# A two-layer graph kernel on one core: weights' block sums on one engine at a time, c on ScalarE, h sums in another order

## The chip, the core and the metric

The kernel runs on one core of a Trainium2 chip. A core has a matrix engine (TensorE, PE in the profile) and three engines that work element by element: VectorE (DVE), ScalarE (ACT) and GpSimd (POOL). SyncE (SP) issues most transfers. Each engine works through its own queue in the order in which the program gives it instructions, and waits for another engine only by semaphores. The metric is the device time of one execution in microseconds (us); "before" is the median of three runs.

## What is computed

The input `x` holds 128 batches of a 128 x 512 matrix. `adj` is a 128 x 128 matrix, mostly zeros.

```python
# layer 0
h = max(layernorm(x), 0)
A = adj @ h; C = A + b                            # (batch, 128, 512)
pre = A[:, :, None, :] + (C - A)[:, :, :, None]
x = x + max over the last axis of relu(pre)       # cut: comes to x + relu(rowmax(A) + b)
# layer 1
h = max(layernorm(x), 0)
q, k, v = h @ Wq + bq, h @ Wk + bk, h @ Wv + bv   # 8 heads of 64
w = softmax(q k^T / 8, masked where adj == 0)
x = x + w @ v
```

The step of layer 0 adds to each row of `x` one number, which the kernel calls `c`; layernorm takes away what is constant in a row, so both layers use the same `h`, and `c` is only added to the result.

## The kernel before

The batches are worked in 32 groups of four (`G = 4`, `NG = 32`). For each group PE makes the scores of the group, its `v`, and the `q` and `k` of the next group, then the attention of the group. The three projections are done in the manner of Strassen and Winograd: `h` and the weights are cut in quarters, sums of quarters are formed, and seven products take the place of eight. Most of these seven are cut once more in the same way, so that sums of blocks of 128 x 128 are needed too.

Sums of the weights are made once, in the beginning. A `weight_blocks` of one `k` is four additions of 128 x 128; there are five `k` for each of the three weights.

```python
def weight_blocks(eng, n, ks=(3, 2, 0, 1, 4)):
    for k in ks:
        ...                                        # (cut) a: a quarter or sum, s: the four results
        for o, x, op, y in (
            (s[0], a[:, 1, 0], ALU.add, a[:, 1, 1]),
            (s[2], s[0], ALU.subtract, a[:, 0, 0]),
            (s[1], a[:, 0, 0], ALU.subtract, a[:, 1, 0]),
            (s[3], a[:, 0, 1], ALU.subtract, s[2]),
        ):
            eng.tensor_tensor(o, x, y, op=op)      # L422
```

Sums of `h` are made for every group. `h_sum(g, k)` is one of four subtractions over quarters (512 columns): `t3 = b22 - b12`, `t1 = b12 - b11`, `t2 = b22 - t1`, `t4 = b21 - t2` for k = 0 to 3. `h_blocks(g, k, parts)` forms, on GpSimd, the block sums of one of `t4 b22 b21 t1 t3` (k = 0 to 4) in three parts; part 0 has 256 columns, parts 1 and 2 have 128.

```python
eng.tensor_tensor(HB[g][o], HB[g][a], HB[g][b], op=ALU.subtract)     # h_sum, L379
nc.gpsimd.tensor_tensor(o, x, y, op=ALU.subtract)                    # h_blocks, L396
```

The number `c` of a batch is made from the row maximum of its adjacency product; `add_bv` adds the bias of `v` to `x` on GpSimd, and `add_c` adds `c` on ScalarE.

```python
def maximum(m):
    g, i = divmod(m, G)
    nc.vector.reduce_max(AMAX[g][:, i : i + 1], PA[m], axis=AX.X)    # L352
    if i == G - 1:
        nc.vector.tensor_scalar(C[g], AMAX[g], b0_sb, 0.0, op0=ALU.add, op1=ALU.max)   # L354

def norm_end(m, bv=True):
    nc.scalar.activation(HN[m], x_of(m), AF.Relu, scale=RSTD[m], bias=NMR[m])          # L308
    if m >= G and bv:
        add_bv(m)                                                    # L314, GpSimd
```

The products of one projection of one group stand in six rows, and after each row come the other engines' tasks of that row (`todo`). `first`, `sixth`, `seventh` and `inner` are matmuls of blocks on PE (L587); what ends in `_to` is the DVE work that takes their results out of PSUM (L639, L665); `end...` is DVE or ScalarE work that finishes a product of quarters (L517, L521, L527).

```python
def steps(p, tail, mid, t3):
    t = tail + [lambda: None] * 8
    return [
        [t[0], p.p1],
        [call(p.first, 5, True), call(p.first_to, 5), t[1], call(p.p6a, (0,)), ...],       # cut
        [call(p.first, 2, True), call(p.seventh, 7), call(p.seventh_to, 7), call(p.terms7, 0), mid,
         call(p.inner, 2), p.end2, call(p.inner, 5), call(p.first43), call(p.first_to, 2),
         call(p.first_to, 4),
         call(p.inner, 7), t3, call(p.terms7, 1)],
        [p.end7, p.end5],
        [call(p.sixth, 2), call(p.sixth_to, 2), call(p.sixth, 4), call(p.sixth, 3), call(p.sixth_to, 4)],
        [call(p.inner, 4), call(p.inner, 3), call(p.seventh, 2), call(p.seventh, 4),
         call(p.seventh, 3), call(p.seventh_to, 2), call(p.seventh_to, 4), p.end4],
    ]
```

`p6a` is the product that uses `t2`. The `v` of group 0 and of group 31 and the first `k` are done without the second cut: seven products of quarters, each eight matmuls of 256 columns (L481), in the order `p1, p6, p2, p7, p5, p4, p3`; `p7` waits until DVE's `end6` (L517) has read the bank of `p6`, `p4` in the same way for `end7` (L517), `p3` for `end5` (L527).

The beginning and the tasks of a group:

```python
weight_sums(nc.gpsimd, "v")                      # four sums over 512 columns, L434
plain_q(0, 0)
weight_sums(nc.vector, "k")
...                                              # cut: norms, adjacency, plain_q, products of the first k
weight_sums(nc.gpsimd, "q")
weight_blocks(nc.gpsimd, "q", (3,))
for g in range(NG):
    ...                                          # cut
    add(4, h_sum, g + 1, k)                      # k = 1, 2; on VectorE
    for k, i in ((4, 0), (4, 1), (3, 0), (3, 1)):
        add(4, h_blocks, g + 1, k, (i,))
    add(5, h_sum, g + 1, 3, nc.gpsimd)
    for k, i in ((2, 0), (3, 2), (2, 1), (2, 2), (0, 0), (1, 0), (4, 2)):
        add(5, h_blocks, g + 1, k, (i,))
    ...                                          # cut
    if g == 0:
        for s, k in enumerate((3, 2, 0, 1, 4)):
            add(s, weight_blocks, nc.vector, "k", (k,))
        for s, k in ((0, 2), (0, 0), (1, 1)):
            add(s, weight_blocks, nc.vector, "q", (k,))
        for s, k in ((0, 3), (0, 2), (1, 0), (1, 1), (2, 4)):
            add(s, weight_blocks, nc.vector if k in (3, 2) else nc.gpsimd, "v", (k,))
        add(3, weight_blocks, nc.gpsimd, "q", (4,))
        for i in range(G):
            add((3, 3, 3, 11)[i], add_bv, i)
```

Of the kernel before, what the change touches and what calls it, by code (L numbers as in the profile page):

```python
# [53 lines left out]
G = 4  # L54
# [115 lines left out]
def tile_adj_preln_d2(  # L170
# [42 lines left out]
    def fast(ctx):  # L213
# [136 lines left out]
        def maximum(m):  # L350
            g, i = divmod(m, G)
            nc.vector.reduce_max(AMAX[g][:, i : i + 1], PA[m], axis=AX.X)  # L352
            if i == G - 1:
                nc.vector.tensor_scalar(C[g], AMAX[g], b0_sb, 0.0, op0=ALU.add, op1=ALU.max)  # L354

        def adjacency(m):
            product(m)
# [338 lines left out]
                    return  # L696
                self.add_blocks(k, 1, slice(0, 2), 7)

        def steps(p, tail, mid, t3):

            t = tail + [lambda: None] * 8
            return [
                [t[0], p.p1],
                [call(p.first, 5, True), call(p.first_to, 5), t[1], call(p.p6a, (0,)),
                 call(p.first, 7, True), call(p.first_to, 7), call(p.p6a, (1, 2)),
                 call(p.sixth, 5), call(p.sixth_to, 5), call(p.sixth, 7), call(p.sixth_to, 7),
                 call(p.p6a, (3,)), call(p.seventh, 5), call(p.seventh_to, 5), p.end6],
                [call(p.first, 2, True), call(p.seventh, 7), call(p.seventh_to, 7), call(p.terms7, 0), mid,
                 call(p.inner, 2), p.end2, call(p.inner, 5), call(p.first43), call(p.first_to, 2),
                 call(p.first_to, 4),  # L710
                 call(p.inner, 7), t3, call(p.terms7, 1)],
                [p.end7, p.end5],
                [call(p.sixth, 2), call(p.sixth_to, 2), call(p.sixth, 4), call(p.sixth, 3), call(p.sixth_to, 4)],
                [call(p.inner, 4), call(p.inner, 3), call(p.seventh, 2), call(p.seventh, 4),
                 call(p.seventh, 3), call(p.seventh_to, 2), call(p.seventh_to, 4), p.end4],
            ]

        def later(p):
# [2 lines left out]
        def call(m, *a):  # L721
            return lambda: m(*a)
# [119 lines left out]
        with tc.manual_schedule():  # L842
# [11 lines left out]
            adjacency(1)  # L854
            transposes(2)
            transposes(3)
            weight_sums(nc.gpsimd, "v")
            plain_q(0, 0)
            weight_sums(nc.vector, "k")
# [1 line left out]
                h_sum(0, k)  # L861
            adjacency(2)
            norm(G)
            norm_end(G)
            plain_q(0, 1)
            norm(G + 1)
            norm_end(G + 1)
            adjacency(3)
            plain_q(1, 0)
            blocks(G)  # L870
            blocks(G + 1)
            move(G + 1)
            plain_q(1, 1)
            k = Products(0, "k")
            more = {
# [5 lines left out]
            for s, p in enumerate((k.p1, k.p6, k.p2, k.p7, k.p5, k.p4, k.p3)):  # L881
                p()
                for f, m in more.get(s, ()):
                    f(m)
            weight_sums(nc.gpsimd, "q")
            weight_blocks(nc.gpsimd, "q", (3,))
            for g in range(NG):
                b = g * G
                if g > 0:
# [3 lines left out]
                for p in [Products(g, "v")] + [Products(g + 1, n) for n in "qk" if g + 1 < NG]:  # L893
                    if p.n == "v" and g in (0, NG - 1):
                        part += [
                            [p.p1], [p.p6], [p.p2], [p.p7], [p.p5], [p.p4, p.p3],
                        ]
                        continue
                    t3 = mid = lambda: None
                    if p.n == "v":  # L900
                        t3 = lambda: h_sum(g + 1, 0, nc.gpsimd)
                    if p.n == "q":
                        mid = lambda: [
                            h_blocks(g + 1, k, (i,)) for k, i in ((0, 1), (1, 1), (0, 2), (1, 2))
                        ]
                    part += steps(p, tail, mid, t3)
                    tail = later(p)
                    if p.n == "k":
                        part[-1] += tail
                        tail = []  # L910
# [6 lines left out]
                if g + 1 < NG:  # L917
# [9 lines left out]
                        add(0, adjacency, m - 1)  # L927
                    if g == 0:
                        add(3, h_sum, 1, 0)
                    for k in (1, 2):  # L930
                        add(4, h_sum, g + 1, k)
                    for k, i in ((4, 0), (4, 1), (3, 0), (3, 1)):
                        add(4, h_blocks, g + 1, k, (i,))
                    add(5, h_sum, g + 1, 3, nc.gpsimd)
                    for k, i in ((2, 0), (3, 2), (2, 1), (2, 2), (0, 0), (1, 0), (4, 2)):
                        add(5, h_blocks, g + 1, k, (i,))
                    if g + 2 < NG:
                        for s, l in next_norms(m).items():
# [25 lines left out]
                for s, ps_ in enumerate(part):  # L964
                    for p in ps_:
                        p()
# [51 lines left out]
```

## Time and profile before

| what | value |
|---|---|
| median of 3 runs | 1506.74 us |
| lowest and highest | 1502.37 and 1508.06 us |
| span of the profiled execution | 1497.8 us |
| PE busy | 1473.3 us, 98% |
| POOL busy | 1317.3 us, 88% |
| DVE busy | 1217.8 us, 81% |
| ACT busy | 652.7 us, 44% |

A row of a timeline has the start in us from the beginning of the span, the duration in us, the engine, the line of the kernel, the operation, what it writes and reads, the shapes and how many equal instructions are merged into the row. In brackets stand the engine's idle time before the row and what ended it. A matmul of float32 appears as two instructions. Matmuls overlap in the pipe, so the distance of two starts tells what one costs PE, and the duration of a row is longer than that. A row of windows has the stretch, its length, then for each engine its busy time and its number of instructions, then the clock, the share of the DMA engines and what they moved.

### The profile page before, as it was taken

To read this page: it belongs to the slowest core of one execution; us is meant where nothing else is said; L and a number is where in the kernel's file an instruction comes from. 1 tells how busy PE (TensorE), PEld (TensorE's weight loads), DVE (VectorE), ACT (ScalarE), POOL (GpSimd) and SP (SyncE) were. 2 spreads that over 40 slices of the span, in tenths; PEclk is the share of its full clock that TensorE was granted. 3 is DMA by queue.
4 is the path that set the end of the run, shared out by engine and by line. 5 is a ranking of instruction groups with operands and counts; after the bars stand their busy time and mean duration, and the time that the engine had idled before them with its cause. 6 is when DMAs were issued, how large, how long until landed. Compare 5 with 4: busy or idle time off the path is not lost.

```text
span 1497.8 us, 38618 instructions
## 1 busy us (share of the span) xinstructions
PE 1473.3 (98%) x14565; PEld 1336.5 (89%) x14565; DVE 1217.8 (81%) x3016; ACT 652.7 (44%) x1455; POOL 1317.3 (88%) x1564
## 2 busy tenths in 40 slices
PE   8899999999999999999999999999999999999997
PEld 6789998999898999999998999999999989999987
DVE  6988877888788888788887888887888878888877
ACT  3344444444544444444445444444444454444432
POOL 5799899899898898998988988989989889889882
PEclk9999999999999999999999999999999999999999
DMA  5231223312223212233122232122332222331211
GB/s 172 48 86 27 75 76 82 86 37 70 76 77 86 66 43 77 75 83 86 30 76 74 79 86 70 40 78 75 82 86 40 67 74 77 86 79 33 63 42 59
DMA packets 307836, 105.67 MB, mean 71 GB/s; under 512 B 273152, under 2 KB 273280, under 8 KB 307648
## 3 DMA queue, kind: packets, MB, share of 16 engines
q1 hardware_dynamic: 307328, 102.84, 26.6%
q8 instruction: 117, 1.92, 0.5%
q14 instruction: 71, 0.58, 0.1%
q0 software_dynamic: 176, 0.27, 0.1%
q10 hardware_dynamic: 144, 0.07, 0.0%
HBM read 37.03 MB, written 33.55 MB: 47 GB/s over the span
## 4 chain that ended last, share of the span: by engine, by line
PE 93%; DVE 3%; POOL 2%; issue 1%; DMA 0%; ACT 0%; SPq 0%; DVEq 0%; POOLq 0%
PE bk L587 47%; PE bk L481 22%; PE bk L786 8%; PE bk L756 8%; PE bk L348 7%; PE bk L732 1%; POOL h L396 1%; DMA xp<-in_x_dram 0%; DVE ssk_sb L422 0%; POOL w L768 0%; POOL xp L314 0%; POOL o L816 0%; POOL u L690 0%; DVE ssq_sb L422 0%; DVE amax L352 0%
## 5 line engine op out<-in xcount | busy, mean ns | idle before, releaser
L768 POOL TENSOR_TENSOR w<-w,live 128x512 f32<-128x512 f32 x248 | 308.5, 1276 | 0.0
L690 POOL TENSOR_TENSOR u<-u,t 128x512 f32<-128x512 f32 x184 | 234.4, 1274 | 82.0 <-DVE t L639 57.0
L764 ACT ACTIVATE w<-bk 128x512 f32<-128x512 f32 x256 | 128.8, 628 | 276.3 <-PE bk L756 276.3
L665 DVE TENSOR_TENSOR u<-u,bk 128x256 f32<-128x256 f32 x552 | 206.5, 415 | 43.6 <-PE bk L587 26.6
L639 DVE TENSOR_TENSOR u<-u,bk 128x128 f32<-128x128 f32 x368 | 109.0, 316 | 81.8 <-PE bk L587 80.8
L816 POOL TENSOR_TENSOR o<-xp,o 128x512 f32<-128x512 f32 x122 | 151.8, 1277 | 20.1 <-DVE RS L803 20.1
L314 POOL TENSOR_TENSOR xp<-xp,bv_sb 128x512 f32<-128x512 f32 x128 | 159.4, 1278 | 3.7 <-ACT hn L308 3.7
L308 ACT ACTIVATE hn<-xp,nmr,rstd 128x512 f32<-128x512 f32 x124 | 100.5, 811 | 137.4 <-POOL nmr L305 82.4
L352 DVE TENSOR_REDUCE amax<-bk 128x1 f32<-128x512 f32 x128 | 86.6, 677 | 77.2 <-PE bk L348 77.2
L508 ACT COPY u<-bk 128x512 f32<-128x512 f32 x95 | 55.0, 579 | 184.0 <-PE bk L481 176.2
L348 PE MATMUL bk<-hn,adjT 128*128 128x512 f32 x248 | 126.9, 593 | 0.0
L786 PE MATMUL bk<-v,w 128*64 128x65 f32 x4096 | 126.5, 223 | 0.0
L786 PEld LDWEIGHTS bk<-v,w 128*64 128x64 f32 x4096 | 122.1, 138 | 4.1 <-issue 0.3
L756 PE MATMUL bk<-qT,kT 64*128 64x128 f32 x2048 | 123.0, 275 | 0.0
L756 PEld LDWEIGHTS bk<-qT,kT 64*128 64x128 f32 x2048 | 116.8, 188 | 2.5 <-issue 0.3
L587 PE MATMUL bk<-ssv_sb,h 128*128 128x128 f32 x720 | 111.7, 277 | 0.3 <-DVE u L665 0.3
L587 PEld LDWEIGHTS bk<-ssv_sb,h 128*128 128x128 f32 x720 | 98.6, 192 | 14.5 <-issue 13.9
L804 DVE TENSOR_TENSOR o<-bk,RS 128x448 f32<-128x448 f32 (+1 forms) x161 | 93.7, 582 | 5.5
L812 ACT ACTIVATE xp<-xp,c 128x512 f32<-128x512 f32 x128 | 91.2, 715 | 5.3 <-POOL xp L314 5.3
L321 DVE STREAM_TRANSPOSE tb<-hn 128x512 f32<-128x512 f32 x124 | 87.0, 702 | 2.4 <-ACT hn L308 2.4
L396 POOL TENSOR_TENSOR h<-hT,h 128x128 f32<-128x128 f32 x186 | 83.7, 457 | 4.9
L587 PEld LDWEIGHTS bk<-h,ssq_sb 128*128 128x128 f32 x558 | 74.7, 192 | 14.9 <-issue 7.2
(201 smaller groups left out, 4101.4 us busy)
## 6 DMA issues: line engine op xcount, KB each, us to landing
out_dram<-o SPq DMA_DIRECT2D x128, 256.0 KB, 2.4
xp<-in_x_dram SPq DMA_DIRECT2D x62, 512.0 KB, 5.1
hT<-tb SPq DMA_DIRECT2D x992, 32.0 KB, 1.9
xp<-in_x_dram SPq DMA_DIRECT2D x4, 256.0 KB, 4.1
wq_sb<-in_L_gnn_Wq_dram SPq DMA_DIRECT2D x2, 512.0 KB, 7.5
wk_sb<-in_L_gnn_Wk_dram SPq DMA_DIRECT2D x2, 512.0 KB, 9.5
wv_sb<-in_L_gnn_Wv_dram SPq DMA_DIRECT2D x2, 512.0 KB, 10.5
bv_sb<-in_L_gnn_bv_dram POOLq DMA_DIRECT2D x1, 256.0 KB, 6.8
```

The lines of the kernel that those rows point to most:

```text
L314: nc.gpsimd.tensor_tensor(x_m, x_m, bv_sb, op=ALU.add)
L348: nc.tensor.matmul(PA[m], adjT, HN[m], start=True, stop=True)
L481: nc.tensor.matmul(bank[:, r, :], lhs, rhs, start=first and i == 0, stop=i == 3, skip_group_check=True,)
L587: nc.tensor.matmul(out, lhs, rhs, start=start, stop=True, skip_group_check=True)
L639: nc.vector.tensor_tensor(to, to, what.to_broadcast(to.shape), op=ALU.add)
L665: nc.vector.tensor_tensor(to, to, what, op=ALU.add)
L690: nc.gpsimd.tensor_tensor(u, u, T7, op=ALU.add)
L756: nc.tensor.matmul(psc[j][:, f, :], KT[g][r, f, i * D : (i + 1) * D], QT[g][r, f, i * D : (i + 1) * D], start=True, stop=True,)
L764: nc.scalar.activation(w[:, j], psc[j], AF.Exp, scale=HD ** -0.5)
L768: eng.tensor_tensor(w[:, j], w[:, j], live_h, op=ALU.mult)
L786: nc.tensor.matmul(pav[r, c : c + HE], w[:, h % 2, h // 2, r], V[:, i, h, :], start=True, stop=True,)
L816: eng.tensor_tensor(y, x_of(b), y, op=ALU.add)
```

## The change

The changed kernel computes the same with the same instructions but for `c`; it moves them to other engines and places.

- **Weights' block sums.** Those of `v` are now all on VectorE, in the beginning, beside the products of the first `k`. Those of `k` stay on VectorE beside the `v` products of group 0, and those of `q` are all on GpSimd. They are to share the element engines better, and no stretch is to have sums of all three weights at once.
- **Bias additions.** `add_bv` of batches 0 to 3 goes to the beginning, ahead of the sums of Wv on GpSimd; that of batches 4 and 5 goes behind the first products.
- **c on ScalarE.** One activation (Relu with bias) takes the place of VectorE's `tensor_scalar`.
- **Second sum of h.** `h_sum(g + 1, 2)`, which makes `t2`, goes from row 4 to a place just ahead of `end4` in the last row of `v`, behind `seventh_to`, so that VectorE empties PE's bank first.
- **GpSimd's block sums.** All three parts of `b21` (k = 2) come ahead of `t4 = b21 - t2`, since `t2` comes later.
- **The last full group.** In group 30, where no adjacency products are left, `first43` is issued before `inner(5)`.

```diff
-                nc.vector.tensor_scalar(C[g], AMAX[g], b0_sb, 0.0, op0=ALU.add, op1=ALU.max)
+                nc.scalar.activation(C[g], AMAX[g], AF.Relu, bias=b0_sb)
...
-                 call(p.inner, 2), p.end2, call(p.inner, 5), call(p.first43), call(p.first_to, 2),
-                 call(p.first_to, 4),
+                 call(p.inner, 2), p.end2] + [call(p.inner, 5), call(p.first43)][::-1 if late else 1] +
+                [call(p.first_to, 2), call(p.first_to, 4),
...
-                 call(p.seventh, 3), call(p.seventh_to, 2), call(p.seventh_to, 4), p.end4],
+                 call(p.seventh, 3), call(p.seventh_to, 2), call(p.seventh_to, 4)] + ([t2, p.end4] if p.n == "v" else [p.end4]),
...
+            for m in range(G):
+                add_bv(m)
             weight_sums(nc.gpsimd, "v")
...
             blocks(G)
+            weight_blocks(nc.vector, "v", (3, 2, 0))
             blocks(G + 1)
             move(G + 1)
+            weight_blocks(nc.vector, "v", (1, 4))
...
+                if s < 2:
+                    add_bv(G + s)
+                elif s < 6:
+                    weight_sum(nc.gpsimd, "q", s - 2)
-            weight_sums(nc.gpsimd, "q")
-            weight_blocks(nc.gpsimd, "q", (3,))
+            weight_blocks(nc.gpsimd, "q", (3, 2))
...
+                        t2 = lambda: h_sum(g + 1, 2)
...
-                    part += steps(p, tail, mid, t3)
+                    part += steps(p, tail, mid, t2, t3, g == NG - 2)
...
-                    for k in (1, 2):
-                        add(4, h_sum, g + 1, k)
+                    add(4, h_sum, g + 1, 1)
+                    if g == 0:
+                        add(4, h_sum, 1, 2)
...
+                    add(5, h_blocks, g + 1, 2)
                     add(5, h_sum, g + 1, 3, nc.gpsimd)
-                    for k, i in ((2, 0), (3, 2), (2, 1), (2, 2), (0, 0), (1, 0), (4, 2)):
+                    for k, i in ((0, 0), (1, 0), (3, 2), (4, 2)):
                         add(5, h_blocks, g + 1, k, (i,))
...
-                    for s, k in enumerate((3, 2, 0, 1, 4)):
+                    add(0, weight_blocks, nc.gpsimd, "q", (0, 1, 4))
+                    for s, k in ((0, 3), (0, 2), (1, 0), (1, 1), (3, 4)):
                         add(s, weight_blocks, nc.vector, "k", (k,))
-                    for s, k in ((0, 2), (0, 0), (1, 1)):
-                        add(s, weight_blocks, nc.vector, "q", (k,))
-                    for s, k in ((0, 3), (0, 2), (1, 0), (1, 1), (2, 4)):
-                        add(s, weight_blocks, nc.vector if k in (3, 2) else nc.gpsimd, "v", (k,))
-                    add(3, weight_blocks, nc.gpsimd, "q", (4,))
-                    for i in range(G):
-                        add((3, 3, 3, 11)[i], add_bv, i)
```

More of the change, by code (lines that the diff above doesn't have):

```diff
@@ L697, in seventh_to, with steps @@
                 self.add_blocks(k, 1, slice(0, 2), 7)
-        def steps(p, tail, mid, t3):
+        def steps(p, tail, mid, t2, t3, late):
             t = tail + [lambda: None] * 8
@@ L863, in fast @@
             norm(G)
-            norm_end(G)
+            norm_end(G, False)
             plain_q(0, 1)
             norm(G + 1)
-            norm_end(G + 1)
+            norm_end(G + 1, False)
             adjacency(3)
@@ L898, in fast @@
                         continue
-                    t3 = mid = lambda: None
+                    t2 = t3 = mid = lambda: None
                     if p.n == "v":
+                        t2 = lambda: h_sum(g + 1, 2)
                         t3 = lambda: h_sum(g + 1, 0, nc.gpsimd)
```

## The prediction

> **What bounds the kernel now.** I read the page's busy shares and the chain that ended last first, then a table of windows cut at the first score matmul (L756) of each group of four batches, then the timelines of the stretches that stood out.
>
> ```profile
> PE 1473.3 (98%) x14565; PEld 1336.5 (89%) x14565; DVE 1217.8 (81%) x3016; ACT 652.7 (44%) x1455; POOL 1317.3 (88%) x1564
> ...
> PE 93%; DVE 3%; POOL 2%; issue 1%; DMA 0%; ACT 0%; SPq 0%; DVEq 0%; POOLq 0%
> ```
>
> TensorE (PE) is the bound: a saving elsewhere counts only where PE waits for it. The windows show where that is: columns are the stretch, its length, then busy time by engine.
>
> ```profile
> 44.39:96.14 51.75, 46.21 (x427) 40.75 (x427) 48.10 (x113) 19.74 (x43) 43.67 (x64) 1.00 0.18 40
> 96.14:142.69 46.55, 45.87 (x462) 41.54 (x458) 38.62 (x95) 20.59 (x46) 41.60 (x50) 1.00 0.27 69
> 142.69:188.34 45.65, 45.61 (x463) 41.65 (x459) 37.38 (x95) 20.48 (x46) 41.61 (x50) 1.00 0.29 71
> 1378.04:1423.68 45.64, 45.60 (x463) 41.63 (x459) 37.36 (x95) 20.48 (x46) 41.60 (x50) 1.00 0.24 59
> ```
>
> A group takes 45.64 us when nothing disturbs it. The first costs 51.75 us, 6.1 more, and in it DVE is busy 48.10 of them. From the starts of the other groups' first score matmuls, most intervals are 45.63 to 45.69; six are longer: 46.55, 46.03, 46.63, 46.67 and twice 45.88.
>
> In the first group, on PE:
>
> ```profile
> 51.72 1.89 PE L481 MATMUL bk<-wv_sb,hT 128*128 128x256 f32 x8
> 55.55 1.97 PE L481 MATMUL bk<-sv_sb,hs 128*128 128x256 f32 x8 [1.94 <-DVE u L517]
> ...
> 61.60 2.00 PE L481 MATMUL bk<-wv_sb,hs 128*128 128x256 f32 x8 [1.50 <-DVE u L517]
> 64.98 1.97 PE L481 MATMUL bk<-sv_sb,hT 128*128 128x256 f32 x8 [1.39 <-DVE v L527]
> ...
> 71.58 0.69 PE L587 MATMUL bk<-h,wq_sb 128*128 128x128 f32 x4 [0.71 <-DVE u L639]
> ```
>
> Eight such matmuls issue in 1.73 us (50.00 to 51.72), so the row at 55.55 starts 2.10 us late (51.72 + 1.73 = 53.45). In the same way 61.60 is 1.66 late, 64.98 is 1.65 late and 71.58 is 0.88 late. The sum is 6.3 us. Each waits for a DVE instruction that stands in DVE's queue behind the weights' block sums (L422). The L517 that releases 55.55 ran at 54.73, after 20 block sums without a gap from 47.28 to 54.73: 0.37 us each.
>
> **What the Trainium skill says.** The page "SBUF — State Buffer", section "Who interferes with whom": VectorE and GpSimd share a pair of SBUF ports under an exclusive lock; a VectorE tensor_scalar that runs on two ports, and a VectorE instruction with two SBUF inputs against a GpSimd one that reads SBUF, block or are blocked; PE and ScalarE wait for nobody. The trace agrees. `c` is a tensor_scalar over 4 columns: 0.229 us at best, 0.534 median, 1.82 at worst, each time beside GpSimd work:
>
> ```profile
> 103.53 1.82 DVE L354 TENSOR_SCALAR c<-amax,b_sb 128x4 f32<-128x4 f32 x1
> ...
> 101.55 3.73 POOL L816 TENSOR_TENSOR o<-xp,o 128x512 f32<-128x512 f32 x3
> ...
> 105.59 0.49 PE L587 MATMUL bk<-wv_sb,h 128*128 128x128 f32 x2 [0.64 <-DVE u L639]
> ```
>
> It ends when GpSimd's run ends (101.55 + 3.73 = 105.28), and PE pays. Block sums of 128x128 have two SBUF inputs: 0.28 us alone, 0.4 to 0.6 beside GpSimd, up to 1.35 beside its 512-column additions. Second place: the page "ScalarE: Activation LUTs", section "Rules for kernel authors", budgets about 0.3 us for an activation with a pointer bias plus 0.83 ns per element; for 4 columns that is an estimate of 0.3 us, and no run so far shows this shape. Relu already runs in this kernel, whose one table load is at the beginning.
>
> **Part 1, the weights' block sums.** There are 60 (three weights, five sets of four). Before, DVE did 40 of them in the congested stretch and GpSimd 20. Now GpSimd does the 20 of q, DVE does the 20 of k there, and DVE does the 20 of v earlier, between 26 and 31.6 us. There DVE has room: it is idle from 26.5 to 28.9 and from 29.6 to 31.6, 4.4 us; GpSimd is idle then too, so the 20 should run at about 0.21 us each (the spacing of the rows at 47.81 and 48.01), 4.2 us. They fit; PE, which runs without a wait from 13 to 44 us, should not notice. In the v products DVE then has 8 k-sums (about 3 us with contention, 46.2 to 49.2) before its first L517, which PE makes ready at 51.7: no wait. The later k-sums, 8 and then 4, lie in the 1.7 us or more between PE's deadlines. GpSimd gives up seven bias additions (1.28 us each) to earlier idle time and gets the 12 remaining q-sums until about 58.4; the additions to `x` of batches 0 to 3 fill its wait for Wv up to 16.85. The q products begin near 61 instead of 66.78, so the h block sums on GpSimd, from 58.4, still keep ahead. All four waits should go: 6.3 us, of which I count 6.0.
>
> **Part 2, c on ScalarE.** Half a microsecond of DVE per group is free on most groups, since PE doesn't wait there. It counts in the three with 1.8 us: 46.55, 46.63 and 46.67 less 45.64 is 0.91, 0.99 and 1.03. Sum 2.9; I count 2.7. ScalarE is idle there (its copy at 102.42 ends at 103.0, the next starts at 104.18).
>
> **Part 3, the second sum of h.** On the way from v to q, in every group:
>
> ```profile
> 158.95 0.83 DVE L379 TENSOR_TENSOR hT<-hT 128x512 f32<-128x512 f32 x1
> 159.81 0.83 DVE L379 TENSOR_TENSOR hs<-hT 128x512 f32<-128x512 f32 x1
> 160.57 0.41 DVE L639 TENSOR_TENSOR v<-v,bk 128x256 f32<-128x256 f32 x1
> 160.90 0.74 DVE L665 TENSOR_TENSOR u<-u,bk 128x256 f32<-128x256 f32 x2
> ...
> 161.34 0.44 PE L587 MATMUL bk<-h,wq_sb 128*128 128x128 f32 x2
> 161.82 0.46 PE L587 MATMUL bk<-hT,sq_sb 128*128 128x128 f32 x2
> ...
> 173.88 0.38 PE L587 MATMUL bk<-h,wk_sb 128*128 128x128 f32 x2
> 174.10 0.39 PE L587 MATMUL bk<-hT,sk_sb 128*128 128x128 f32 x2
> ```
>
> From q to k the pair of rows stands 0.22 apart; from v to q it stands 0.48 apart. The second row writes the scratch bank that L639 and L665 read, and these end at 161.64 because both h sums stand before them. With the second sum (159.81) behind them they end near 160.9, ahead of PE. That returns 0.26 us in 30 groups (1 to 30), 7.8 at most. But the sum now ends near 161.63, and its result `t2` feeds the product at 162.11, which moves up to 161.85: only 0.2 us remains for the semaphore. I count 0.2 x 30 = 6.0.
>
> **Part 4, GpSimd's other order.** The sums of `b21` come before `t4` since `t4` needs `t2`; same instructions, same sum. The last sum that inner(5) of q needs, (3,2), moves from 164.06 to about 166.0, and its matmul is at 166.74 before: 0.4 us in hand after the shift. I count 0, with a risk.
>
> **Part 5, the last full group.** Two waits for DVE L665 (1437.67 and 1462.37) make PE 0.45 us late each, since no adjacency product stands there to fill the time. Issuing first43 before inner(5) puts three matmuls (0.67 us) between. I count 0.9. The waits for GpSimd there (0.5) may stay.
>
> **Sum.** 6.0 + 2.7 + 6.0 + 0.9 = 15.6; less 0.8 for small waits that I can't place (part 4's above all): 14.8. 1506.7 - 14.8 = 1491.9.
>
> **Rivals.** First, part 3 gives nothing: `t2` becomes the wait, because DVE's sum is stretched beside GpSimd (0.83 instead of 0.69 already, 0.99 at one place), or (3,2) arrives late. For it speaks the 0.2 us margin; against it that the lost time is then at most what it was. Result 1506.7 - 8.8 = 1497.9, and with 0.1 us of new wait in each group 1501. Second, the waits of the beginning move rather than go: q's sums, all on GpSimd and slowed by DVE's k-sums at its side, delay the h block sums, and PE waits for GpSimd at 61 to 68 us. GpSimd is busy 43.67 of the first 51.75 us, so it has about 2 us to spare in 45.7. Half of part 1 would be lost: about 1495. Third, GpSimd becomes the bound: busy 41.6 of 45.4 us, with room of 3.8 us per group and its waits for DVE inside that; I give it little.
>
> **Range and chances.** The best sum, 6.3 + 2.9 + 7.8 + 1.5, is 18.5 and gives 1488; rivals one and two together give about 1501. The three times before spread over 5.7 us, so 1485 to 1500 should hold it 8 times in 10. For faster by over 2% it would need under 1476.6, twice the sum that PE's waits allow: 0.03. Slower by over 2% would need a new wait of 1 us in every group: 0.02. Within 2%: 0.95.
>
> **What would show it.** First interval of score matmuls 45.7 to 46.2 (before 51.75) and no PE row in it with a wait for L517; `c` on ACT near 0.2 to 0.3 us and no interval above 46; a plain group at 45.38 to 45.45 with the v-to-q pair 0.22 apart; the group before the last 0.9 shorter. I am wrong if the product with `t2` or inner(5) of q starts late in every group, if PE waits for GpSimd L396 in the first group, or if the early v-sums hold back DVE so that PE waits before 44 us.

## The result and the profile after

| | before | after |
|---|---|---|
| median | 1505.72 us (1502.37 to 1508.06, 4 runs) | 1493.96 us (1492.89 to 1494.99, 4 runs) |
| span of the profiled execution | 1497.8 us | 1491.1 us |
| first interval of score matmuls | 51.75 us | 45.23 us |
| a plain interval | 45.64 us | 45.75 us |

The ratio is 0.9923, with a 95% interval of 0.9902 to 0.9945: 11.8 us less, and within the range predicted. The spans of the profiled executions differ by 6.7 us only. Both numbers have to be explained, and the parts of the sum as well.

The page of the changed kernel, engines and chain that ended last:

```profile
PE 1473.0 (99%) x14565; PEld 1343.2 (90%) x14565; DVE 1184.2 (79%) x2984; ACT 661.4 (44%) x1487; POOL 1318.0 (88%) x1564
...
PE 78%; POOL 18%; DVE 2%; issue 1%; DMA 1%; ACT 0%; SPq 0%; DVEq 0%; POOLq 0%
```

PE is as busy as before and GpSimd too, but GpSimd's share of the chain went from 2% to 18%. The windows of the changed kernel, cut at the same matmuls as before (stretch, length, then busy time of PE, weight loads, DVE, ACT, POOL):

```profile
45.89:91.12 45.23, 45.23 (x428) 40.98 (x427) 38.16 (x92) 19.75 (x43) 41.68 (x62) 1.00 0.20 47
136.86:182.62 45.76, 45.69 (x462) 41.87 (x459) 36.54 (x94) 20.78 (x47) 41.60 (x50) 1.00 0.28 70
1417.78:1463.18 45.40, 44.58 (x456) 41.09 (x452) 34.49 (x86) 15.22 (x35) 38.80 (x39) 1.00 0.13 35
```

The first group lost its 6.5 us of waiting. All the plain intervals now lie between 45.72 and 45.77, with none above 46, but a plain one is 0.11 longer than a plain one before. The last full group is 0.26 shorter. The first score matmul, on the other hand, comes at 45.89 instead of 44.39.

The beginning in the changed kernel, PE rows:

```profile
36.23 1.99 PE L481 MATMUL bk<-hs,sk_sb 128*128 128x256 f32 x8 [1.01 <-DVE u L521]
...
43.14 1.10 PE L348 MATMUL bk<-hn,adjT 128*128 128x512 f32 x2 [0.61 <-DVE amax L352]
```

These are two new waits, ahead of the part that I had looked at. The first row is 1.17 us late and the second 0.77, by the usual distances of PE starts. The reason of the first is on DVE, the reason of the second on GpSimd:

```profile
14.25 1.64 DVE L434 TENSOR_TENSOR sk_sb<-sk_sb,wk_sb 128x512 f32<-128x512 f32 x1
...
16.41 1.75 DVE L434 TENSOR_TENSOR sk_sb<-wk_sb,sk_sb 128x512 f32<-128x512 f32 x1
...
36.87 2.50 POOL L314 TENSOR_TENSOR xp<-xp,bv_sb 128x512 f32<-128x512 f32 x2 [0.93 <-ACT hn L308]
39.31 0.55 POOL L289 TENSOR_TENSOR rstd<-ve,mhalf 128x1 f32<-128x1 f32 x1
```

Two of the four sums of Wk took 0.69 us before and 1.64 and 1.75 now: at their side stand the four early `add_bv` on GpSimd (9.90 to 15.34) and then the Wv sums. DVE runs 1.6 us later from there on (its first `L284` after the sums starts at 24.44 instead of 22.82), so the `v` sums, 28.03 to 33.53, no longer fit ahead of the `L521` that PE waits for, which starts at 35.30 instead of 33.35. Later the two `add_bv` of batches 4 and 5 stand in GpSimd's queue ahead of the `rstd` of batch 7, and the normalized rows of that batch come 2.8 us later (the ACT row of L308 at 40.26 instead of 37.42).

The way from `v` to `q` in a plain group of the changed kernel, PE and GpSimd:

```profile
155.50 0.38 PE L587 MATMUL bk<-h,wq_sb 128*128 128x128 f32 x2
155.72 0.39 PE L587 MATMUL bk<-hT,sq_sb 128*128 128x128 f32 x2
...
160.35 0.39 PE L587 MATMUL bk<-hT,wq_sb 128*128 128x128 f32 x2
160.81 0.49 PE L587 MATMUL bk<-h,sq_sb 128*128 128x128 f32 x2
...
155.82 0.72 POOL L396 TENSOR_TENSOR h<-hT 128x256 f32<-128x256 f32 x1
156.62 0.99 POOL L396 TENSOR_TENSOR h<-hT,h 128x128 f32<-128x128 f32 x2
157.57 1.27 POOL L379 TENSOR_TENSOR hs<-hT,hs 128x512 f32<-128x512 f32 x1
158.92 0.73 POOL L396 TENSOR_TENSOR h<-hs 128x256 f32<-128x256 f32 x1
159.61 0.73 POOL L396 TENSOR_TENSOR h<-hT 128x256 f32<-128x256 f32 x1
160.30 0.46 POOL L396 TENSOR_TENSOR h<-hT,h 128x128 f32<-128x128 f32 x1
```

The pair of PE rows stands 0.22 us apart, as predicted. But at 160.35 + 0.22 = 160.57 PE is ready for inner(5) of `q`, and starts it at 160.81: (3,2), the last row, ends at 160.76. The waits view has this in all thirty groups: `PEld bk L587` for `POOL h L396`, 7.6 us. (The kernel before has 7.9 us of waits of that name too, but mostly at the first product of `q`, where PE came only 0.06 us later by them.) The time saved is spent a few rows later, and some more.

### The profile page after: what moved, and what is told of

Same layout as the page of the kernel before. It is cut to its first block, busy times and chain, and to the rows that moved or that the text cites. A ratio compares the mean times of both kernels' runs of the same rounds, so it can differ in the third digit from the quotient of the medians.

```text
span 1491.1 us, 38616 instructions
## 1 busy us (share of the span) xinstructions
PE 1473.0 (99%) x14565; PEld 1343.2 (90%) x14565; DVE 1184.2 (79%) x2984; ACT 661.4 (44%) x1487; POOL 1318.0 (88%) x1564
## 4 chain that ended last, share of the span: by engine, by line
PE 78%; POOL 18%; DVE 2%; issue 1%; DMA 1%; ACT 0%; SPq 0%; DVEq 0%; POOLq 0%
PE bk L587 38%; PE bk L481 17%; POOL h L396 13%; PE bk L786 8%; PE bk L756 8%; PE bk L348 7%; POOL u L690 3%; POOL hs L379 2%; DMA wk_sb<-in_L_gnn_Wk_dram 1%; DVE sk_sb L434 0%; DVE hs L379 0%; DVE ssv_sb L422 0%; POOL xp L314 0%; ACT hn L308 0%; DVE o L804 0%
## 5 line engine op out<-in xcount | busy, mean ns | idle before, releaser
L768 POOL TENSOR_TENSOR w<-w,live 128x512 f32<-128x512 f32 x248 | 308.6, 1277 | 0.0
L690 POOL TENSOR_TENSOR u<-u,t 128x512 f32<-128x512 f32 x184 | 234.2, 1273 | 76.1 <-DVE t L639 53.2
L665 DVE TENSOR_TENSOR u<-u,bk 128x256 f32<-128x256 f32 x552 | 206.0, 414 | 58.5 <-PE bk L587 35.8
L639 DVE TENSOR_TENSOR u<-u,bk 128x128 f32<-128x128 f32 x368 | 108.9, 316 | 99.7 <-PE bk L587 96.7
L308 ACT ACTIVATE hn<-xp,nmr,rstd 128x512 f32<-128x512 f32 x124 | 100.5, 811 | 157.2 <-POOL nmr L305 97.0
L816 POOL TENSOR_TENSOR o<-xp,o 128x512 f32<-128x512 f32 x122 | 151.8, 1278 | 20.2 <-DVE RS L803 20.2
L587 PE MATMUL bk<-ssv_sb,h 128*128 128x128 f32 x720 | 111.4, 277 | 0.1
L587 PEld LDWEIGHTS bk<-ssv_sb,h 128*128 128x128 f32 x720 | 98.5, 191 | 14.2 <-issue 13.9
L396 POOL TENSOR_TENSOR h<-hT,h 128x128 f32<-128x128 f32 x186 | 96.2, 517 | 7.3
L587 PEld LDWEIGHTS bk<-h,ssq_sb 128*128 128x128 f32 x558 | 75.6, 191 | 15.3 <-DVE u L665 7.7
```

Source lines behind the costliest of these rows:

```text
L587: nc.tensor.matmul(out, lhs, rhs, start=start, stop=True, skip_group_check=True)
L665: nc.vector.tensor_tensor(to, to, what, op=ALU.add)
L690: nc.gpsimd.tensor_tensor(u, u, T7, op=ALU.add)
L768: eng.tensor_tensor(w[:, j], w[:, j], live_h, op=ALU.mult)
L816: eng.tensor_tensor(y, x_of(b), y, op=ALU.add)
```

## The experiments

Theory: the beginning gave some 5 us; `c` more than the profile of before lets one see; the second sum of `h` only opened a wait for GpSimd, which the new order of block sums made longer than the wait removed. The rivals were that the second sum of `h` brings the gain and `c` little, and that the loss per group comes from `t2` itself and not from the order of GpSimd. Intervals are those between the first score matmuls of two groups. Kernels of one session share the runs of the kernel before: a median of 1510.01 us (29 runs) in the first, 1507.59 (11) in the second, 1507.14 (9) in the third.

| kernel | made from | median us | ratio to before [95%] | span us | first score matmul | first / plain interval |
|---|---|---|---|---|---|---|
| c_act | before | 1496.12 | 0.9911 [0.9893, 0.9929] | 1494.2 | 44.08 | 51.95 / 45.64 |
| start_only | before | 1504.65 | 0.9972 [0.9955, 0.9990] | 1503.4 | 47.32 | 45.31 / 45.64 |
| h_only | before | 1510.88 | 1.0005 [0.9996, 1.0014] | 1503.0 | 44.51 | 50.79 / 45.75 |
| old_pool | after | 1488.15 | 0.9859 [0.9842, 0.9877] | 1485.7 | 46.82 | 45.22 / 45.53 |
| early32 | after | 1498.78 | 0.9936 [0.9911, 0.9961] | 1495.8 | 46.23 | 45.22 / 45.87 |
| best | old_pool | 1491.96 | 0.9889 [0.9864, 0.9914] | 1489.9 | 44.41 | 51.89 / 45.51 |
| late_off | after | 1495.21 (one run) | – | 1493.4 | 47.57 | 45.22 / 45.75 |
| before_again | before | 1505.53 (one run) | – | 1503.8 | 44.20 | 51.72 / 45.64 |
| gp_less | old_pool | 1481.07 | 0.9823 [0.9807, 0.9839] | 1479.3 | 47.15 | 45.22 / 45.30 |
| best2 | gp_less | 1478.81 | 0.9813 [0.9796, 0.9830] | 1477.0 | 43.92 | 46.52 / 45.31 |

**c_act: c alone.**

```diff
-                nc.vector.tensor_scalar(C[g], AMAX[g], b0_sb, 0.0, op0=ALU.add, op1=ALU.max)
+                nc.scalar.activation(C[g], AMAX[g], AF.Relu, bias=b0_sb)
```

> The kernel before with part 2 alone: c as an activation on ScalarE. Theory A (long waits of c come at random, and the profile of before happened to show only three of them): the six long intervals go, every interval of score matmuls from the second on is 45.6 to 45.7 us; the profiled span falls by about 4 us, from 1497.8 to about 1494, the median by 7 to 10 us, since ordinary runs have more long waits than the profiled one, and the runs lie closer together than the 5.7 us of before. Theory B (three long waits are the rule): the median falls by 3 to 4 us only, and the spread stays.

Measured: 13.9 us less than before, the largest part of all and more than either theory had, and the four runs lie within 0.7 us, where those of before spread over 10. All 32 activations take 0.28 to 0.30 us. What `c` costs on DVE differs from execution to execution, which the next kernel shows.

**before_again: the kernel before, a second profile** (no edit).

> The kernel before, unchanged, to see another execution's waits for c. Theory A: the number of c instructions of 1.8 us on VectorE changes from run to run; the profile of before with three was a short one, so this one has 5 to 15, each worth 0.8 to 0.9 us to the span (start_only showed 14 and h_only 7 in the steady groups). Rival: three again, and the time of the other runs lies elsewhere.

Measured: ten intervals of 46.5 or more, where the profile before had three. The groups of `c` in this execution and in c_act (count, then least, median and longest in ns):

```profile
L354 DVE TENSOR_SCALAR c<-amax,b_sb x32: 229/559/1824, 26.8 to 1437.0; 128x4 f32<-128x4 f32 x32
```

```profile
L354 ACT ACTIVATE c<-amax,b_sb x32: 282/298/300, 29.1 to 1427.7; 128x4 f32<-128x4 f32 x32
```

Median and maximum say little here: what counts is how many of the 32 are long ones of 1.8 us. From the second group's first score matmul to the start of the last full group the first profile has 1327.54 us and this one 1333.70: 6.16 us for 7 more long ones, 0.88 each. In start_only there were 14, in h_only 7. The number is chance, as far as these runs tell. So the profile on which I predicted is a lucky execution: its own time was 1499.53 us, 7.2 below the median of 1506.74.

The four traces with `c` on DVE show what a long one is. Behind the first two of an execution `c` always falls into a run of GpSimd's additions L816. 86 of 120 end 0.02 to 0.03 us after the end of the addition during which they start. The other 34 end 0.04 to 0.10 us after the end of the next one: they sit through one addition more, 1.27 us.

**start_only: the weights' sums and the bias additions alone** (the changed kernel's beginning, with `c`, the sums of `h` and row 4 as before).

```diff
+            for m in range(G):
+                add_bv(m)
...
+            weight_blocks(nc.vector, "v", (3, 2, 0))
...
+                    add(0, weight_blocks, nc.gpsimd, "q", (0, 1, 4))
+                    for s, k in ((0, 3), (0, 2), (1, 0), (1, 1), (3, 4)):
                         add(s, weight_blocks, nc.vector, "k", (k,))
```

> The kernel after with parts 2 to 5 undone, so the kernel before with the weights' block sums and the bias additions alone in their new places. Both theories: the first interval of score matmuls falls from 51.75 to about 45.3 us, the first score matmul comes about 1.5 us later (45.9 instead of 44.4), long waits for c stay. Theory A (the beginning gives 5 us, c the rest): median 4 to 6 us below before. Theory B (the beginning is the main part of the gain): 8 us or more.

Measured: the median is 5.4 us below that of before (1.5 to 6.8 by the interval of the ratio), as theory A has it. The first interval falls to 45.31, and the first score matmul comes at 47.32. The second group begins at 92.63 us; in before_again it begins at 95.92. That is 3.3 us; in the changed kernel it is 96.14 - 91.12 = 5.0. The difference lies ahead of the first score matmul. Six kernels here have this same beginning, and in all of them that matmul starts 21.45 us, to 0.01, after DVE's first `L284` behind the sums of Wk, which starts between 24.44 us (after) and 26.11 (late_off). It moves with the arrival of Wk, since the first sum starts between 13.52 and 15.16, and with how many of the sums are stretched. So the second group begins between 91.12 and 92.78, and the changed kernel's profile is the best of the six.

**h_only: the second sum of h and GpSimd's order alone** (parts 3 and 4).

```diff
-                 call(p.seventh, 3), call(p.seventh_to, 2), call(p.seventh_to, 4), p.end4],
+                 call(p.seventh, 3), call(p.seventh_to, 2), call(p.seventh_to, 4)] + ([t2, p.end4] if p.n == "v" else [p.end4]),
...
+                    add(5, h_blocks, g + 1, 2)
                     add(5, h_sum, g + 1, 3, nc.gpsimd)
-                    for k, i in ((2, 0), (3, 2), (2, 1), (2, 2), (0, 0), (1, 0), (4, 2)):
+                    for k, i in ((0, 0), (1, 0), (3, 2), (4, 2)):
```

> The kernel before with parts 3 and 4 alone: the second sum of h behind the bank's reads, and all block sums of b21 ahead of t4 on GpSimd. Theory A (the wait that part 3 removes comes back at inner(5) of q, where the block sum (3,2) is late): the v-to-q pair of PE rows is 0.22 us apart, but a plain interval is 45.75, 0.1 longer than before, so the median is 2 to 4 us slower than before. Rival (the two orders gain their 0.26 us per group, and something else in the changed kernel eats it): interval 45.4, median 6 to 8 us faster.

Measured: no gain, 1.0005 [0.9996, 1.0014], and the plain interval of 45.75 that the changed kernel has. The two parts together cost 0.11 us a group. The interval is that of theory A; its loss of 2 to 4 us in the median did not show (0.9 us), and the first interval is 0.96 shorter here than in the profile of before.

**old_pool: the changed kernel with GpSimd's old order.** It undoes part 4 alone.

```diff
-                    add(5, h_blocks, g + 1, 2)
                     add(5, h_sum, g + 1, 3, nc.gpsimd)
-                    for k, i in ((0, 0), (1, 0), (3, 2), (4, 2)):
+                    for k, i in ((2, 0), (3, 2), (2, 1), (2, 2), (0, 0), (1, 0), (4, 2)):
```

> The kernel after with part 4 alone undone: GpSimd makes t4 first and the block sum (3,2) as third, as in the kernel before, while the second sum of h stays in its new place on VectorE. Theory A (part 4's order makes (3,2) late; t2 is ready at about 155.5 in the trace after, before GpSimd comes to t4 at about 155.9): no wait for GpSimd at inner(5) of q, plain interval 45.4 to 45.5 instead of 45.75, median 8 us below the changed kernel, about 1486. Rival (part 3 itself is to blame: t4 waits for t2 and drags all later block sums along): interval 45.7 or more, no gain against the changed kernel.

Measured: 1488.15, with every plain interval at 45.53: 0.22 less than with the new order, 0.11 less than before. Part 4 cost 0.22 us a group. The later `t2` doesn't hold up `t4` on GpSimd: there is no gap before it. GpSimd rows of this kernel from the sums of `t3` to the second `u` of L690:

```profile
153.39 0.72 POOL L396 TENSOR_TENSOR h<-hs 128x256 f32<-128x256 f32 x1
...
156.54 1.27 POOL L379 TENSOR_TENSOR hs<-hT,hs 128x512 f32<-128x512 f32 x1
157.77 0.72 POOL L396 TENSOR_TENSOR h<-hT 128x256 f32<-128x256 f32 x1
158.46 1.39 POOL L396 TENSOR_TENSOR h<-hT,h 128x128 f32<-128x128 f32 x3
159.81 0.73 POOL L396 TENSOR_TENSOR h<-hs 128x256 f32<-128x256 f32 x1
...
164.50 1.26 POOL L690 TENSOR_TENSOR u<-u,t 128x512 f32<-128x512 f32 x1
```

In the old order (3,2) stands between (2,0) and (2,1), and the row after (2,0) starts 0.69 us behind it. In the new order (2,1), which reads (2,0)'s result, follows at once and starts 0.80 behind it (155.82, 156.62). `t4` is followed after 1.23 us by a sum that doesn't read it, and in the new order after 1.35 by one that does. These two make 0.23 of the 0.25 us by which the stretch is longer in the new order. (A row x3 or x2 hides its single starts; within these, too, a sum of 128 columns that reads the one before it starts 0.53 behind it, and 0.41 otherwise.)

**early32: (3,2) ahead of the sums of b21.** If only the late (3,2) cost time, putting it first should remove the wait.

```diff
+                    add(5, h_blocks, g + 1, 3, (2,))
                     add(5, h_blocks, g + 1, 2)
                     add(5, h_sum, g + 1, 3, nc.gpsimd)
-                    for k, i in ((0, 0), (1, 0), (3, 2), (4, 2)):
+                    for k, i in ((0, 0), (1, 0), (4, 2)):
```

> The changed kernel with one block sum moved: (3,2), the last of t1, goes ahead of the three of b21 on GpSimd; the rest of part 4 stays. Theory A (only the place of (3,2) is wrong): no wait of PE for GpSimd L396 at inner(5) of q, plain interval 45.5 like with the whole old order (45.53), median within 1 us of it, about 1488. Rival (the old order helped because t4 and its sums came early): (0,0) and (1,0), which come 0.5 us later still, are waited for in place of (3,2), interval 45.6 to 45.75.

Measured: 45.87, slower than the changed kernel's 45.75, so this theory fell. PE no longer waits for (3,2), and waits later instead:

```profile
165.79 0.39 PE L587 MATMUL bk<-h,ssq_sb 128*128 128x128 f32 x2
166.39 0.71 PE L587 MATMUL bk<-h,ssq_sb 128*128 128x128 f32 x4 [0.21 <-DVE u L665]
```

That `L665` waits for GpSimd's L690. (3,2) reads (3,1)'s result and now follows it directly, which adds another 0.12 us to GpSimd's stretch. This gave the next theory: not one sum but the whole stretch sets the pace. From the first block sum of `t3` to the end of the second L690 GpSimd waits for no other engine, then comes `L665`, then PE.

| kernel | GpSimd's stretch us | plain interval | difference |
|---|---|---|---|
| before | 158.50 to 170.97: 12.47 | 45.64 | 33.17 |
| after | 152.67 to 165.29: 12.62 | 45.75 | 33.13 |
| old_pool | 153.39 to 165.76: 12.37 | 45.53 | 33.16 |
| early32 | 153.14 to 165.88: 12.74 | 45.87 | 33.13 |
| gp_less | 153.49 to 165.50: 12.01 | 45.30 | 33.29 |

Four kernels agree in the difference to 0.04 us. That is a match and no proof; gp_less below tests it, and shows that the match of the kernel before is chance.

**late_off: the changed kernel without part 5.**

```diff
-                    part += steps(p, tail, mid, t2, t3, g == NG - 2)
+                    part += steps(p, tail, mid, t2, t3, False)
```

> The changed kernel with part 5 alone undone (inner(5) ahead of first43 in group 30). Theory A: the interval of the last full group is 45.40 with part 5; without it about 45.7 (its two waits for DVE L665 of 0.45 us come back, and the order is worth 0.3 us and not 0.9, since waits of 0.2 to 0.5 us come up at other places). Rival (part 5 is worth its 0.9 us and something else costs 0.6 there): 46.3.

Measured: the last full group takes 45.68 us, and with part 5 it takes 45.40: 0.28 us. The two waits for `L665` that the prediction names, at the `ssv_sb` row in `v` and the `ssk_sb` row in `k`, are gone with part 5; others stay or come (late_off, then after):

```profile
1433.47 0.71 PE L587 MATMUL bk<-ssv_sb,h 128*128 128x128 f32 x4 [0.28 <-DVE u L665]
1446.05 0.68 PE L587 MATMUL bk<-h,ssq_sb 128*128 128x128 f32 x4 [0.37 <-DVE u L665]
1458.19 0.71 PE L587 MATMUL bk<-h,ssk_sb 128*128 128x128 f32 x4 [0.28 <-DVE u L665]
```

```profile
1446.70 0.71 PE L587 MATMUL bk<-h,ssq_sb 128*128 128x128 f32 x4 [0.34 <-DVE u L665]
1457.04 0.49 PE L587 MATMUL bk<-hs,wk_sb 128*128 128x128 f32 x2 [0.18 <-DVE u L521]
```

Laid beside each other matmul by matmul, the two kernels show where the gain goes. In `v` PE is 0.42 us ahead at the `ssv_sb` row, and 2.4 us later it has lost that again to short waits for L517 and L665. In `q` the wait moves to a later matmul and nothing is won. In `k` 0.28 us are left of 0.36.

**best: old_pool with fewer early bias additions.** Batches 0 and 1 early, 4 to 6 together behind the second step, 2 and 3 in rows 8 and 11 of the first group.

```diff
-            for m in range(G):
+            for m in range(2):
                 add_bv(m)
...
+                    add(8, add_bv, 2)
+                    add(11, add_bv, 3)
```

> The changed kernel with the old order on GpSimd, and two moves of bias additions in the beginning: batches 2 and 3 later (rows 8 and 11 of group 0) instead of early, where GpSimd's additions stand against VectorE's sums of Wk; batches 4 to 6 behind the statistics of batch 7 instead of ahead of them. Theory A (the 1.5 us that the first score matmul comes later are these additions): both PE waits there (for u L521 and for amax L352, together 1.9 us) shrink to under 0.5, first score matmul at 44.3 to 44.9 instead of 46 to 47, median 1 to 2 us below the kernel with the old order alone, about 1486.5. Rival (the early v-sums themselves hold VectorE up): the waits stay, first score matmul after 45.5.

Measured: a miss, 1491.96 where old_pool has 1488.15. The beginning is mended (the first score matmul at 44.41, the only wait 0.47 us at 35.59): with two early `add_bv` fewer, all four sums of Wk take 0.68 to 0.69 us again. But the first interval is 51.89. The rows of this kernel that show why (ScalarE, DVE, PE):

```profile
77.93 0.72 ACT L812 ACTIVATE xp<-xp,c 128x512 f32<-128x512 f32 x1 [7.14 <-POOL xp L314]
...
80.72 0.56 ACT L508 COPY u<-bk 128x512 f32<-128x512 f32 x1
...
81.32 0.48 DVE L639 TENSOR_TENSOR u<-u,bk 128x128 f32<-128x128 f32 x2 [4.30 <-ACT u L508]
...
81.66 0.49 PE L587 MATMUL bk<-h,wk_sb 128*128 128x128 f32 x2 [3.43 <-DVE u L639]
```

ScalarE's `add_c` of batch 2 waits 7.14 us for its `add_bv`, which stands behind GpSimd's masks (L768). Behind it in ScalarE's queue stands the copy that DVE needs, and behind that PE. One addition placed too late holds three engines. The interval is 6.67 us longer than in old_pool: 0.71 at the first product of `q`, which waits for block sums of GpSimd that come late, 3.59 at the last row shown, 0.63 just behind it, where PE waits for ScalarE's L676, and 1.74 in the next matmuls, 17 of which start 0.10 us further apart than in old_pool although PE shows no idle time there. So theory A was right about the beginning, and the median missed by what the additions of batch 2 do in the first group; best2 moves these.

**gp_less: old_pool with one block sum of every group moved from GpSimd to VectorE.** (4,2) is the sum; DVE makes it in row 2 of `q`, where it has room.

```diff
                         mid = lambda: [
-                            h_blocks(g + 1, k, (i,)) for k, i in ((0, 1), (1, 1), (0, 2), (1, 2))
+                            h_blocks(g + 1, 4, (2,), nc.vector),
+                            *(h_blocks(g + 1, k, (i,)) for k, i in ((0, 1), (1, 1), (0, 2), (1, 2))),
                         ]
...
-                    for k, i in ((2, 0), (3, 2), (2, 1), (2, 2), (0, 0), (1, 0), (4, 2)):
+                    for k, i in ((2, 0), (3, 2), (2, 1), (2, 2), (0, 0), (1, 0)):
```

> The changed kernel with GpSimd's old order, and one block sum of every group (t3's last, 128x128) taken from GpSimd and given to VectorE, which stands idle for 0.4 us at that place. Theory C (from v to q each interval is paced by GpSimd's chain of work without a gap, from the block sums of t3 to the second addition of L690: 12.47 us in the kernel with c alone and interval 45.64, 12.39 and 45.53 with the old order, 12.61 and 45.75 in the changed kernel, 12.74 and 45.87 with (3,2) early): the chain falls to about 12.0 us and the interval by what PE still waits for it, 0.2 us, to 45.3; median 5 to 7 us below the kernel with the old order. Theory A' (the chain only matters where a block sum comes after its matmul, and with the old order none does): interval stays at 45.5.

Measured: 45.30 in nearly every plain group (45.40 at most), 0.23 less than old_pool, by moving one sum of 0.42 us of 50 GpSimd instructions. The window of the third group:

```profile
137.68:182.99 45.31, 45.31 (x463) 41.63 (x459) 36.88 (x95) 20.78 (x47) 41.18 (x49) 1.00 0.29 71
```

The stretch got 0.36 shorter, the interval 0.23: the remaining 0.13 is where GpSimd stops being the limit. Where the time was lost is told by the starts of the same matmuls in old_pool and here:

```profile
166.03 0.97 PE L587 MATMUL bk<-h,ssq_sb 128*128 128x128 f32 x6
166.83 1.89 PE L481 MATMUL bk<-hT,wk_sb 128*128 128x256 f32 x8
```

```profile
166.13 0.83 PE L587 MATMUL bk<-h,ssq_sb 128*128 128x128 f32 x6
166.80 1.89 PE L481 MATMUL bk<-hT,wk_sb 128*128 128x256 f32 x8
```

The first takes 0.80 us to the next row in old_pool, where a matmul of it waits for `L665` behind the second L690, and 0.67 here: 0.13. Another 0.10 goes at the start of `k`, where PE waits for ScalarE's L676; ScalarE works without a longer gap up to it from an L308 that waits for GpSimd's L305, right behind the stretch. For the changed kernel with the old order, that GpSimd set the pace is therefore shown by taking work away from it, and not only read from the match.

The third group of the other kernels, laid beside this one matmul by matmul, says what each plain interval above 45.30 is made of. The changed kernel loses 0.34 us at inner(5) of `q`, waiting for (3,2), and 0.12 in the two places just named. early32 loses 0.49 and 0.08 in those two places. The kernel before loses 0.35, all of it at the pair of rows on the way from `v` to `q`, and nothing behind GpSimd's stretch: its match in the table is chance. So the pair did cost 0.35 us a group, and this kernel, which has part 3 and less work on GpSimd, is the one in which all of it comes back.

**best2: gp_less with a mended beginning.** As in best, but `add_bv` of batch 2 in row 9, and `add_c` of batch 2 moved behind it to row 13.

```diff
-                    add((2, 5, 9, 15)[i] if g + 1 < NG else i + 1, add_c, b + i)
+                    add((2, 5, 9 if g else 13, 15)[i] if g + 1 < NG else i + 1, add_c, b + i)
                 if g == 0:
+                    add(9, add_bv, 2)
+                    add(11, add_bv, 3)
```

> The same, with the moves of bias additions in the beginning, and batch 2's addition on GpSimd (and its c on ScalarE) later still: in the former attempt ScalarE stood 3 us waiting for that addition behind GpSimd's masks, and PE waited 3.6 us in the first interval. Expected if that was the cause: first score matmul at 44.4, first interval 45.0 to 45.4 instead of 51.89, median 2 us below the kernel without these moves, about 1481. If the first interval stays above 48, something else in the beginning is the cause.

Measured: 1478.81, the fastest of all, with a ratio of 0.9813 [0.9796, 0.9830].

```profile
43.92:90.44 46.52, 46.08 (x428) 41.02 (x427) 38.84 (x93) 19.65 (x43) 45.00 (x64) 1.00 0.21 47
90.44:135.75 45.31, 45.31 (x462) 41.63 (x459) 36.81 (x95) 20.91 (x47) 40.93 (x49) 1.00 0.27 70
```

The median is 2.3 us below gp_less, as expected; the first interval, 46.52, is not the 45.0 to 45.4 expected. The second group begins at 90.44 us; in gp_less it begins at 92.37. In the first group PE is 1.29 us later than in gp_less: 0.17 in `v`, 0.55 from 62.92 on, at the first product of `q`, which waits for GpSimd, and 0.57 from 84.29 on, where it waits for DVE's L521.

## Why the prediction was right, and which steps of it were not

The time was right, 1491.9 predicted and 1493.96 measured, but by luck: two errors of opposite sign hid each other, `c` counted far too low and the sums of `h` counted as a gain where they were a loss. Two of the three signs of being wrong came true: inner(5) of `q` starts late in every group, and PE waits before 44 us. The sum by its terms, in profiled executions:

| term | predicted us | in the profiles us | from |
|---|---|---|---|
| beginning | -6.0 | -5.0 | start of the second group, 96.14 to 91.12 |
| c | -2.7 | -3.3 | second group to last full group, before 1327.54 to c_act 1324.25 |
| second sum of h and GpSimd's order | -6.0 | +2.4 | the same stretch, c_act 1324.25 to after 1326.66 |
| last full group | -0.9 | -0.3 | 45.66 to 45.40 |
| small waits | +0.8 | – | |
| end | – | -0.5 | last group's first score matmul to the end of the span, 28.43 to 27.95 |
| sum | -14.8 | -6.7 | |

The medians fell by 11.8 and not by 6.7, since the profiled execution of before lies 6.2 us below its median of 1505.72, an estimated seven long `c` of 0.88 us fewer, and that of the changed kernel only 1.1 below its own: 6.6 between their times, plus 6.2, less 1.1. The 1.1 fits the spread of the beginning (start_only), which is not shown for these runs.

- **Part 1** was right in its mechanism: all four waits (two for L517, one each for L527 and L639) went, 6.5 us in the first interval. The step that failed is "PE, which runs without a wait from 13 to 44 us, should not notice". I found room on DVE from 26 to 31.6 us in the old trace, and did not follow what the early `add_bv` do to DVE before it: the Wk sums stretched from 0.69 to 1.64 and 1.75 us, and the room came 1.6 us later. The Trainium skill had it on the page that I cited, "SBUF — State Buffer", section "Who interferes with whom" (a VectorE instruction with two SBUF inputs contends with a GpSimd one that reads SBUF), and these rows agree. I had used it for the group's sums only. The wait at 43.14 comes from the order of GpSimd's queue. Net 5.0 instead of 6.0 in this profile, and 3.4 to 4.7 by the second group's start in the five others with this beginning.
- **Part 2** was right in its mechanism and undersized. "Sum 2.9; I count 2.7" fits the profile (3.3), but I took it from a median of other executions. At 0.88 us each, the 7.2 us between the profiled execution and the median are an estimated 8 more long ones. Then the term is some 10 us, and c_act measured 13.9 against a session median of 1510.01. The budget of the page "ScalarE: Activation LUTs", section "Rules for kernel authors", gave 0.3 us; measured 0.28 to 0.30.
- **Part 3** was right that the pair costs time in every group and would close to 0.22 us; in gp_less all of that comes back, 45.30 against 45.64. The step that failed is the path behind it: "I count 0.2 x 30 = 6.0" takes PE to be free up to the next group. With GpSimd's old order 0.11 a group returns (old_pool), then PE waits behind GpSimd's stretch; with the new order nothing returns (h_only, 1.0005). `t2` was not the obstacle.
- **Part 4** failed as a step: "(3,2) moves from 164.06 to about 166.0 ... 0.4 us in hand". At 164.06 (3,2) is over, and the new number is where it begins (161.73 + 1.52 for the sums of `b21` + 1.23 + 2 x 0.69 = 165.86), 0.46 before its end. And it begins 4.48 us behind the first sum of `b21` (155.82 to 160.30) where this working has 4.13, since three sums follow one whose result they read, at 0.11 to 0.12 each. That puts its end near 166.7 instead of 166.0, and 0.4 in hand became 0.24 late.
- **Rival one** came in its second form, "(3,2) arrives late", with 0.11 us of new wait in each group. Its 1501 did not come, since `c` gave so much more than 2.7. "The lost time is then at most what it was" was wrong by that 0.11.
- **Rival three**, GpSimd as the bound, is what part 3 ran into, and I gave it little because of "busy 41.6 of 45.4 us, with room of 3.8 us". The room lies elsewhere in the group. Where it counts, GpSimd works for 12.5 us without waiting for anyone.
- **Part 5**: both waits went, but PE waits soon after for DVE in `v` and in `k`, so that 0.28 us are left instead of 0.9. The step that failed is that nothing else would hold PE there.
- **Rival two** did not come: no PE row of the first group waits for GpSimd L396 in the changed kernel. In best2, whose GpSimd has more to do there, one does, for 0.27 us.

Still open is what decides whether one `c` on DVE sits through a second addition of GpSimd: the same program gave 3 in one execution and 10 in another. The moment of its start doesn't tell: the long ones start 0.74 to 0.78 us into the first addition, and so do most of the short ones (0.73 to 0.78). No run tried to steer it.

## What to carry to other kernels

Before working out savings from a profile, compare the time of the profiled execution with the median; where they lie 7 us apart, as here, the difference is time that the profile does not show, and a wait that comes by chance is a candidate. An engine's busy share over a group doesn't say that it is free: look for the stretch that it works without waiting for others, and see what stands at its end. A wait taken from the busiest engine pays only up to the next such stretch: count what comes after it before counting the wait. When an engine works at such a stretch, leave an independent instruction between one and the next that reads its result, and when room is found for added work, follow first what the other moves do to the engine ahead of that room.

## What was not expected of the hardware

- `c`, 128 x 4 elements on VectorE, took between 0.23 us, where nothing ran on GpSimd beside it, and 1.82, and the number of long ones changed between executions of the same program (3 and 10 of 32). A long one ended just after the second of GpSimd's additions beside it, a short one just after the first. The same on ScalarE took 0.28 to 0.30 us every time.
- On GpSimd, a block sum that reads the result of the one directly before it started 0.11 to 0.12 us later than one that doesn't, whatever the size: 0.53 instead of 0.41 us behind a sum of 128 columns, 0.80 instead of 0.69 behind one of 256, 1.35 instead of 1.23 behind one of 512.
